# Layer 1's weights, biases and key tables prepared in the experts' block, in a pool of their own at the other end of SBUF

## The chip, the cores and the metric

The kernel runs on one core of one Trainium2 chip. The metric is the device time of one execution, in microseconds. Three runs of the kernel before took 2543.7, 2549.39 and 2550.09 us, the median is 2549.39 us. One more execution was taken with the hardware profiler. All rows of the trace below come from that one.

The engines are named as in the profile: PE (TensorE's matmuls), PEld (its weight loads), DVE (VectorE), ACT (ScalarE), POOL (GpSimd) and SP (SyncE, which here issues DMAs).

## The reference

The model has four layers over x of shape 4 x 512 x 128 (B, S, D). Each layer adds a cross attention onto a context of 77 tokens and then a feed-forward part. What matters here is the end of layer 0 and all of layer 1:

```python
x = x + _L0_ffn_ref(_layernorm(x), ln_gamma, ln_beta, Wr, W12, W3)       # 8 experts, top 2
x = x + _L1_xcond_ref(_layernorm(x), ctx_1024, ctx_1024, tau, delta, Wq, bq, Wk, ...)
x = x + _L1_ffn_ref(_layernorm(x), w1, conv_w, conv_b, w2)
x = x + _L2_xcond_ref(ctx_1024, _layernorm(x), _lenS2, condB_pt, W_a, W_c)
...
# _L1_ffn_ref: linear layers with ternary weights and quantised activations
scale = 1.0 / clip(mean(abs(w)), 1e-5);  wq = clip(round(w * scale), -1, 1) / scale
h = bit_linear(x, w1); h = depthwise_conv1d(h, conv_w, conv_b); h = silu(h); return bit_linear(h, w2)
# _L2_xcond_ref: mask = (idx < max(p_t-16, 0)) | (idx > min(p_t+16, src_len))
# gauss = exp(-(idx - p_t)**2 / 128); align = softmax(score) * gauss
```

Two things of this depend on the weights and on four numbers per batch alone, not on x. The first is layer 1's ternary weights, multiplied by the three taps of the convolution and turned, together with the convolution's bias. The second is layer 2's window: the mask, the bell `gauss`, and the keys W_a times context. The kernel calls the first `bit_weights` (L1165) and the second `window_tables` (L1386).

## The kernel before, in words

The work is cut into blocks, one after the other. In each, `with planned() as plan` collects pieces, and `Plan.run` writes them out in an order of its own when the block ends. A piece names the pieces it comes after, the PSUM banks or buffers it takes and uses, and a cost for each engine that may do it. Of all pieces that could start, the planner takes the one with the earliest start. Of those with one start it takes the one with the longest path of costs behind it, and it gives the piece to the engine that would be done first. Costs are in units of about 10 ns, and each engine has a fixed lag on top (30 for PE, 10 for DVE, 250 for a DMA). There are eight PSUM banks. A bank is held from the piece that takes it until the last piece that uses it has been written out. The result is a fixed order on each engine: every engine works through its own queue in that order and waits wherever an operand isn't ready.

The blocks, with their times in the trace:

- **Layer 0's cross attention and routing** (0 to about 164 us), inside `first_part`. POOL sends each token's row to the table `sent` by indirect DMA (`scatter`, L1017).
- **Layer 0's experts** (about 164 to 294 us), also in `first_part`, in the pool `m0w`. For each of eight experts SP fetches 640 rows (`xe`, L1048), PE turns them (L1104), ACT applies gamma and beta (`xTe`, L1559). Then come eight steps of two products (L1565, L1566), a Silu on ACT (L1569) and a product on DVE (`times`, L1572), five output products (L1583), a weighting on DVE (`ye`, L1131), and an indirect DMA by POOL that sends the rows to the table `back`. `xe`, `to` (the rows' destinations, L1089), `hT` and `ye` have two buffers each, so the third expert needs what the first has finished with. In the trace the experts go in pairs: sixteen steps, then ten output products. In this block stands also `context(plan, wp, 1)` (L614): the keys and values of layer 1's cross attention. It has no predecessors, so the planner puts it first.
- **Layer 1** (about 294 to 513 us), `middle_part`. `collect` (L1142) fetches the rows of `back` per batch (L1152) and adds them to x (L1158). For each batch follow the norm (`xa_st` L534, `xa_rs` L544 and L545, `xa_n` L550), the transposes (L568), their copy `xa_t` (L302), the queries (L683), the scores (L698, L703), their maxima on DVE (L711), the logits (L755, L757), the exponentials (L763), the sums and means (L773, L782), the quotient `shares` (L302) and the residual. Then come `bit_ffn`, `window_attention`, and the transposes into Y. The weights of `bit_ffn` and the tables of `window_attention` are made in the same block, in the pool `b1`, which is opened last.
- **The local transformer** (513 us to about 2250 us) and **layer 3** (the rest), which the diff doesn't touch.

What `bit_weights` does: SP loads w1, w2, the taps and the bias (L1178 to L1181). DVE splits the bias into three bf16 terms (`three_terms`, L321 to L328). `ternary` sums the absolute values (DVE L1203), spreads the sum over the partitions (PE L1206), and rounds (DVE L1209 to L1215). Three times DVE multiplies by a tap (`wj`, L1229), PE turns the result (L1233), and ACT or DVE copies it to w1T (L302). At last w2 is turned (L1245) and copied. What `window_tables` does: SP loads two small vectors (L1398, L1399). DVE computes bounds, mask and exponent (L1402 to L1415), ACT the bell (Exp, L1418), PE the keys (L1421), DVE their product with the mask (L1424).

Silu needs another activation table on ACT than Exp. The changes are ACT_TABLE_LOAD rows in the trace: one before the experts' first Silu, one before layer 1's first Exp.

A pool that is opened where an older one has been closed can be written only when everything in that older pool has been used for the last time.

Of the kernel before, what the change touches and what calls it, by code (L numbers as in the profile page):

```python
# [238 lines left out]
def tile_kernel(ctx: ExitStack, tc: tile.TileContext, A: dict, out: bass.AP):  # L239
# [922 lines left out]
        return last  # L1162


    def bit_weights(plan, mp):  # L1165

        w1, w2 = (mp.tile([128, NFC, 128], F32, name=f"bw{k}") for k in range(2))
        cw = mp.tile([128, NFC, 3], F32, name="cw")
        cb = mp.tile([128, FF], BF16, name="cb")
        w1T = mp.tile([128, 3, FF], F32, name="w1T")  # L1170
        w2b = mp.tile([128, NFC, 128], BF16, name="w2b")
        w2T = mp.tile([128, NFC, D], BF16, name="w2T")
        out_scale = mp.tile([128, 1], F32, name="out_scale")
        magic = mp.tile([128, 2], F32, name="magic")
        row = plan.buf(mp, [128, FF], F32, "cbrow", 1)

        def load(e):
            e.dma_start(w1, A["L1_ffn_w1"].rearrange("(c p) d -> p c d", p=128))  # L1178
            e.dma_start(w2, A["L1_ffn_w2"].rearrange("d (c f) -> d c f", f=128))
            e.dma_start(cw, A["L1_ffn_conv_w"].rearrange("(c p) o j -> p c (o j)", p=128))  # L1180
            e.dma_start(row.t, A["L1_ffn_conv_b"].partition_broadcast(128))  # L1181

        def magics(e):
            e.memset(magic[:, 0:1], MAGIC)
            e.memset(magic[:, 1:2], -MAGIC)

        loaded = plan.add(load, takes=[row], Q=200)
        done = [plan.add(magics, G=30, V=20)]
        for k in range(4):
            def terms(e, k=k):  # L1190
                at = slice(128 * k, 128 * k + 128)
                three_terms(cb[:, at], row.t[:, at], mp, [128, 128], e)

            done.append(plan.add(terms, [loaded], uses=[row], V=120))

        def ternary(w, scale):

            part = mp.tile([128, 1], F32, name=f"tn_part{w is w2}")
            r = mp.tile([128, 1], F32, name=f"tn_r{w is w2}")
            bank = plan.bank()  # L1200

            def total(e):
                e.tensor_reduce(part, w, AX.XY, ALU.add, apply_absolute_value=True)  # L1203

            def spread(e):
                e.matmul(bank.view(128, 1), ones, part, start=True, stop=True)  # L1206

            def rounded(e):
                e.tensor_scalar(scale, bank.view(128, 1), 1.0 / (FF * D), 1e-5, ALU.mult, ALU.max)  # L1209
                e.reciprocal(r, scale)  # L1210
                e.tensor_scalar(w, w, r, MAGIC, ALU.mult, ALU.add)
                e.tensor_scalar(w, w, MAGIC, 1.0, ALU.subtract, ALU.min)
                e.tensor_scalar(w2b if w is w2 else w, w, -1.0, None, ALU.max)
                if w is w2:
                    e.tensor_scalar(scale, scale, 1.0 / 254.0, None, ALU.mult)  # L1215

            p = plan.add(total, [loaded], V=68)
            p = plan.add(spread, [p], takes=[bank], PE=15)
            return plan.add(rounded, [p], uses=[bank], V=200)

        m1 = mp.tile([128, 1], F32, name="tn_m")
        t1, t2 = ternary(w1, m1), ternary(w2, out_scale)

        for j in range(3):
            bank, wj = plan.bank(), plan.buf(mp, [128, NFC, D], F32, "wj")

            def tap(e, j=j, wj=wj):
                for c in range(NFC):
                    e.tensor_scalar(wj.t[:, c], w1[:, c], m1, cw[:, c, j : j + 1], ALU.mult, ALU.mult)  # L1229

            def flip(e, bank=bank, wj=wj):
                for c in range(NFC):
                    e.transpose(bank.view(128, NFC, 128)[:, c], wj.t[:, c], ident)  # L1233

            def out(e, j=j, bank=bank):
                copy(e, w1T[:, j], bank.view(128, FF))

            p = plan.add(tap, [t1], takes=[wj], V=112)
            p = plan.add(flip, [p], takes=[bank], uses=[wj], PE=54)
            done.append(plan.add(out, [p], uses=[bank], S=59, V=69))  # L1240
        bank = plan.bank()

        def flip2(e):
            for c in range(NFC):
                e.transpose(bank.view(128, NFC, 128, dtype=BF16)[:, c], w2b[:, c], identb)  # L1245

        def out2(e):
            copy(e, w2T, bank.view(128, NFC, 128, dtype=BF16))

        p = plan.add(flip2, [t2], takes=[bank], PE=26)  # L1250
        done.append(plan.add(out2, [p], uses=[bank], S=59, V=69))
        return done, w1T, w2T, cb, out_scale, magic
# [130 lines left out]
        return last  # L1383


    def window_tables(plan, kp):  # L1386

        pt = kp.tile([128, B], F32, name="pt")
        leni = kp.tile([128, B], I32, name="leni")
        end, st, pe = (kp.tile([128, B], F32, name=n) for n in ("end", "st", "pe"))  # L1390
        keep, gauss, wk = (kp.tile([128, B, SK], F32, name=n) for n in ("keep", "gauss", "wk"))
        neg = kp.tile([128, B, SK], BF16, name="neg")
        above = kp.tile([128, SK], F32, name="above")
        idx = cst[:, C_IDX : C_IDX + SK]
        bank = plan.bank()

        def load(e):
            e.dma_start(pt, A["condB_pt"].partition_broadcast(128))  # L1398
            e.dma_start(leni, A["_lenS2"].partition_broadcast(128))  # L1399

        def bounds(e):
            e.tensor_copy(end, leni)  # L1402
            e.tensor_scalar(st, pt, 16.0, 0.0, ALU.subtract, ALU.max)
            e.tensor_scalar(pe, pt, 16.0, None, ALU.add)
            e.tensor_tensor(end, pe, end, ALU.min)

        def inside(e, b):
            e.tensor_scalar(keep[:, b], idx, st[:, b : b + 1], None, ALU.is_ge)
            e.tensor_scalar(above, idx, end[:, b : b + 1], None, ALU.is_le)
            e.tensor_tensor(keep[:, b], keep[:, b], above, ALU.mult)  # L1410
            e.tensor_scalar(gauss[:, b], idx, pt[:, b : b + 1], None, ALU.subtract)

        def outside(e):
            e.tensor_scalar(neg, keep, 1.0, cst[:, C_BIG : C_BIG + 1], ALU.subtract, ALU.mult)
            e.tensor_tensor(gauss, gauss, gauss, ALU.mult)  # L1415

        def bell(e):
            e.activation(gauss, gauss, AF.Exp, scale=-1.0 / 128.0)  # L1418

        def keys(e):  # L1420
            e.matmul(bank.view(128, B, SK), wT[:, 12], ctxT, start=True, stop=True)  # L1421

        def kept(e):
            e.tensor_tensor(wk, bank.view(128, B, SK), keep, ALU.mult)  # L1424

        p = plan.add(bounds, [plan.add(load, Q=80)], V=64)
        for b in range(B):
            p = plan.add(lambda e, b=b: inside(e, b), [p], V=96)
        p = plan.add(outside, [p], V=90)
        done = [plan.add(bell, [p], S=46)]  # L1430
        q = plan.add(keys, takes=[bank], PE=60)
        done.append(plan.add(kept, [p, q], uses=[bank], V=48))
        return done, wk, neg, gauss
# [79 lines left out]
        return last  # L1513


    def first_part():

        with ExitStack() as es:
            pool = lambda name, bufs=2: es.enter_context(tc.tile_pool(name=name, bufs=bufs))
# [4 lines left out]
            with tc.tile_pool(name="xw0", bufs=2) as wp, planned() as plan:  # L1524
# [10 lines left out]
                for e0 in range(E):  # L1535
# [7 lines left out]
                    for g in range(3):  # L1543
# [10 lines left out]

                        p = plan.add(flip, [loaded], takes=[bank], uses=[raw if g < 2 else raw3], PE=58)
                        plan.add(out, [p], uses=[bank], S=60, V=69)
            with tc.tile_pool(name="m0w", bufs=2) as wp, planned() as plan:
                def turn_in(e, dst, t):
                    e.activation(dst, t, AF.Identity, scale=col(R_GAM), bias=col(R_BET))  # L1559
# [25 lines left out]
                sends, issued = experts(  # L1585
                    plan, wp, sent[:1], back[0], CAP0, [], turn_in, hidden, down, R.issued
                )
                context(plan, wp, 1)
            return issued

    def middle_part(issued, Y):

        with ExitStack() as es:
            yp = es.enter_context(tc.tile_pool(name="y0", bufs=2))
            wp = es.enter_context(tc.tile_pool(name="xw1", bufs=2))
            mp = es.enter_context(tc.tile_pool(name="b1", bufs=1))
            with planned() as plan:
                start = collect(plan, yp, back[0], issued, [])
                last = cross_attention(plan, wp, 1, [], start)
                last = bit_ffn(plan, wp, bit_weights(plan, mp), [[p] for p in last])  # L1600
                last = window_attention(plan, wp, window_tables(plan, mp), last)
                for b in range(B):


# [502 lines left out]
    with tc.tile_pool(name="y", bufs=1) as yp:  # L2107
        Y = []
        for b in range(B):
            y = yp.tile([128, S + 1], F32, name=f"y{b}", tag=f"y{b}")  # L2110
            G.memset(y[64:128, 0:1], 0.0)
            Y.append(y)
        with ExitStack() as es:
            open_cross(es)
            middle_part(first_part(), Y)
        local_transformer(Y)
    with ExitStack() as es:
        open_cross(es)
# [20 lines left out]
```

## Time and profile before

| what | value |
| --- | --- |
| median of the runs | 2549.39 us (2543.7 to 2550.09) |
| the profiled execution | 2504.74 us |
| its span, first to last instruction | 2503.0 us |
| mean granted clock of PE | 0.958 |
| PE, DVE, POOL, ACT busy | 90%, 72%, 62%, 50% |
| first xe fetched | 166.81 us |
| first output row sent to `back`, last one sent | 193.35 us, 292.33 us |
| first rows of `back` fetched by SP | 294.53 us |
| local transformer's first load on SP | 513.18 us |

A row of a timeline has the start, the length, the engine, the line of the code, the operation, what is written and read, the shape, and a count. In brackets stands how long the engine had been idle before, and what ended that. A row of stages has the busy time of each engine in that stretch, with the number of instructions in parentheses, then the granted clock of PE as a share of full speed, the DMA engines' share, and GB/s. The profiled execution is about 45 us shorter than the median of the runs.

### The profile page before, as it was taken

The page shows a single profiled execution, that of the slowest core. Times are in us where ns is not written, and L with a number is a line of the kernel's source. Part 1 is how long each engine was busy: PE and PEld are TensorE (multiplying, and loading weights), DVE is VectorE, ACT ScalarE, POOL GpSimd, SP SyncE. Part 2 cuts the span into 40 slices and gives each one's busy share as a digit, 9 for nine tenths or more (in the row PEclk, how much of TensorE's full clock was granted, in tenths as well). Part 3 has the DMA queues.
Part 4 walks back from the last instruction along what each step waited for, and adds up shares of the span by engine and source line. Part 5 has one row for each costly group of instructions (what it writes and reads, how often), then busy time and mean ns, then how long its engine had stood idle before and what let it go on. Part 6 is the DMA issues. An engine that isn't in the chain of part 4 may idle for free.

```text
span 2503.0 us, 87683 instructions
## 1 busy us (share of the span) xinstructions
PE 2254.2 (90%) x37341; PEld 1471.1 (59%) x37341; DVE 1791.1 (72%) x4016; ACT 1243.5 (50%) x2185; POOL 1542.9 (62%) x2613
## 2 busy tenths in 40 slices
PE   7969789968999999999999999999999999978776
PEld 3547534535666666666666666666666666634455
DVE  5543475757887888888888888888888888737522
ACT  3623134534565655556555555565555655514322
POOL 2333312357777777777778777777777777712543
PEclk9979889989999999999999999999999999979888
DMA  6211200026211121111211121111211111111023
GB/s 160 87 31 38 70 1 2 1 58 138 73 35 28 35 69 35 33 28 35 71 34 35 28 78 31 30 32 28 78 32 29 35 28 35 33 29 50 27 68 90
DMA packets 134305, 116.21 MB, mean 46 GB/s; under 512 B 29505, under 2 KB 102700, under 8 KB 133916
## 3 DMA queue, kind: packets, MB, share of 16 engines
q1 hardware_dynamic: 128373, 102.81, 15.8%
q0 software_dynamic: 4608, 7.35, 0.9%
q8 instruction: 296, 4.85, 0.8%
q14 instruction: 93, 0.76, 0.1%
q10 hardware_dynamic: 935, 0.43, 0.1%
HBM read 42.84 MB, written 21.52 MB: 26 GB/s over the span
## 4 chain that ended last, share of the span: by engine, by line
PE 57%; DVE 20%; issue 8%; POOL 7%; ACT 5%; DMA 3%; SPq 1%; ACTq 0%; POOLq 0%; DVEq 0%
PE ps_tr L582 9%; PE ps_mm L1774 8%; PE ps_av L1938 4%; PE ps_tr L1853 4%; PE ps_av L1914 4%; PE ps_sc L1883 3%; DVE rc L1784 3%; DVE rs L1787 3%; DVE ss L1796 3%; PE ps_sc L1984 3%; PE ps_sc L1996 3%; PE ps L1312 2%; DVE P L1894 2%; PE ps L773 2%; DVE la_mx L1893 2%
## 5 line engine op out<-in xcount | busy, mean ns | idle before, releaser
L1797 POOL TENSOR_TENSOR rc<-rc,rs 128x512 f32<-128x512 f32 x384 | 488.6, 1276 | 230.6 <-DVE rs L1787 186.5
L1774 PE MATMUL ps_mm<-wqk,y 128*128 128x512 f32 x768 | 397.5, 600 | 11.0 <-DVE rs L1787 7.8
L1818 POOL TENSOR_TENSOR rc<-rc,rn_y 128x512 f32<-128x512 f32 x384 | 388.8, 1044 | 7.5
L1784 DVE TENSOR_TENSOR rc<-ps_mm,tabs 128x512 f32<-128x512 f32 x384 | 262.4, 683 | 160.9 <-ACT sq L1776 145.6
L1899 ACT ACTIVATE P<-P 128x1024 f32<-128x1024 f32 x96 | 101.4, 1057 | 422.3 <-DVE P L1894 422.3
L1776 ACT ACTIVATE sq<-ps_mm 128x512 f32<-128x512 f32 x384 | 231.0, 602 | 152.3 <-PE ps_mm L1774 104.4
L1787 DVE TENSOR_TENSOR rs<-ps_mm,tabs 128x512 f32<-128x512 f32 x384 | 261.5, 681 | 5.9 <-POOL rc L1797 5.8
L1796 DVE TENSOR_REDUCE ss<-sq 128x8 f32<-128x512 f32 x384 | 259.4, 676 | 0.0
L582 PE MATMUL ps_tr<-cst,rc 128*128 128x128 f32 x1536 | 211.0, 281 | 6.8 <-POOL rc L1818 4.6
L1914 PEld LDWEIGHTS ps_av<-v,PT 64*32 64x32 f32 x12288 | 137.8, 105 | 127.3 <-PE ps_tr L582 54.9
L1938 PE MATMUL ps_av<-aT,wo 128*128 128x128 f32 x1536 | 198.6, 282 | 4.7 <-issue 4.7
L1938 PEld LDWEIGHTS ps_av<-aT,wo 128*128 128x128 f32 x1536 | 179.2, 191 | 14.7 <-issue 6.0
L582 PEld LDWEIGHTS ps_tr<-cst,rc 128*128 128x128 f32 x1536 | 165.4, 141 | 26.2 <-POOL rc L1818 5.7
L1883 PE MATMUL ps_sc<-kT,qT 64*32 64x64 f32 x12288 | 146.7, 225 | 34.5 <-issue 26.9
L1914 PE MATMUL ps_av<-v,PT 64*32 64x65 f32 x12288 | 168.8, 225 | 7.0 <-DVE attn L1924 5.4
L1883 PEld LDWEIGHTS ps_sc<-kT,qT 64*32 64x32 f32 x12288 | 140.2, 105 | 45.2 <-issue 30.9
L1017 POOL DMA_INDIRECT back<-ye,to x80 | 77.6, 970 | 141.7 <-DVE ye L1131 102.5
L1774 PEld LDWEIGHTS ps_mm<-wqk,y 128*128 128x128 f32 x768 | 124.9, 193 | 61.0 <-issue 44.7
L763 ACT ACTIVATE P<-ps,deltaT 77x512 f32<-77x512 f32 x192 | 115.1, 682 | 59.1 <-PE ps L757 58.9
L1830 ACT COPY kT<-ps_tr 128x512 f32<-128x512 f32 x192 | 103.3, 589 | 82.3 <-PE ps_tr L582 82.1
L1830 ACT COPY qT<-ps_tr 128x512 f32<-128x512 f32 x192 | 103.2, 589 | 76.8 <-PE ps_tr L582 74.4
L1924 DVE TENSOR_TENSOR attn<-ps_av,la_den 128x512 f32<-128x512 f32 x192 | 132.8, 691 | 6.6
(392 smaller groups left out, 4453.7 us busy)
## 6 DMA issues: line engine op xcount, KB each, us to landing
v<-v SPq DMA_DIRECT2D x432, 65.0 KB
v<-v SPq DMA_DIRECT2D x96, 195.0 KB
wqk<-in_L_ffn_Wqkv_dram SPq DMA_DIRECT2D x24, 256.0 KB
sent<-xn SPq DMA_DIRECT2D x2, 2210.0 KB
xe<-sent SPq DMA_DIRECT2D x16, 260.0 KB
back<-xn SPq DMA_DIRECT2D x2, 2048.0 KB
raw<-in_L_ffn_W_dram SPq DMA_DIRECT2D x8, 512.0 KB
yb<-back SPq DMA_DIRECT2D x16, 256.0 KB
```

The lines of the kernel that those rows point to most:

```text
L582: PE.transpose(t[:, i], src[:, i], ident)
L1774: PE.matmul(t, lhs, T.w[2 * kind + c], start=True, stop=True)
L1776: SC.activation(sq, t, AF.Square)
L1784: V.tensor_tensor(a, t, bc(T.tabs[:, 2 * kind, tt], [128, 8, LD], 1), ALU.mult)
L1787: V.tensor_tensor(r.rearrange("p h (x d) -> p h x d", x=2), t.rearrange("p h (x d) -> p h x d", x=2)[:, :, ::-1], bc(T.tabs[:, 2 * kind + ...
L1796: V.tensor_reduce(T.ss[:, kind, 8 * c : 8 * c + 8], sq, AX.X, ALU.add)
L1797: G.tensor_tensor(a, a, r, ALU.add)
L1818: G.tensor_tensor(a, a, bc(y[:, o : o + 8], [128, 8, LD], 2), ALU.mult)
L1830: SC.copy(t[:, 4 * c : 4 * c + 4, lead:], to_features(T.rot[kind, c].rearrange("p (k x) d -> p k (x d)", x=2)),)
L1883: PE.matmul(T.banks[32 * w : 32 * w + 32, z, k], T.qT[r, k, 32 * w : 32 * w + 32], T.kT[r, k, 32 * w : 32 * w + 64], start=False, stop=Tru ...
L1914: PE.matmul(T.means[32 * w : 32 * w + 32, x0, k], T.PT[r, 4 * g + k, 32 * w : 32 * w + 32], (T.v1 if w % 2 else T.v2)[r, x0, 4 * g + k], s ...
L1938: PE.matmul(t, T.wo[:, c], T.aT[:, c], start=(c == 0), stop=(c == 7))
```

## The change

The diff does four things.

1. `bit_weights` and `window_tables` are called in the experts' block, after `experts`, and no longer in layer 1's. Layer 1 gets their tiles and an empty list of predecessors.
2. What layer 1 reads later stays in the pool `b1`, which is now opened between the two blocks of `first_part`, on the right side of SBUF (pools are otherwise stacked from the left), and is closed after layer 1. This holds for cb, w1T, w2T, out_scale, magic, wk, neg, gauss and the small vectors.
3. What is needed only while preparing moves into the experts' pool `m0w`. This holds for the raw weights, the taps, w2b, the bias row, wj, the parts of `three_terms`, keep and above.
4. `context(plan, wp, 1)` gets predecessors: those of the fifth send from the end, which is the first send of the last expert.

```diff
-    def bit_weights(plan, mp):
+    def bit_weights(plan, mp, wp):
-        w1, w2 = (mp.tile([128, NFC, 128], F32, name=f"bw{k}") for k in range(2))
-        cw = mp.tile([128, NFC, 3], F32, name="cw")
+        w1, w2 = (wp.tile([128, NFC, 128], F32, name=f"bw{k}", bufs=1) for k in range(2))
+        cw = wp.tile([128, NFC, 3], F32, name="cw", bufs=1)
...
-        w2b = mp.tile([128, NFC, 128], BF16, name="w2b")
+        w2b = wp.tile([128, NFC, 128], BF16, name="w2b", bufs=1)
...
-        row = plan.buf(mp, [128, FF], F32, "cbrow", 1)
+        row = plan.buf(wp, [128, FF], F32, "cbrow", 1)
...
-                three_terms(cb[:, at], row.t[:, at], mp, [128, 128], e)
+                three_terms(cb[:, at], row.t[:, at], wp, [128, 128], e)
...
-            bank, wj = plan.bank(), plan.buf(mp, [128, NFC, D], F32, "wj")
+            bank, wj = plan.bank(), plan.buf(wp, [128, NFC, D], F32, "wj")
...
-    def window_tables(plan, kp):
+    def window_tables(plan, kp, wp):
...
+        keep = wp.tile([128, B, SK], F32, name="keep", bufs=1)
...
+        above = wp.tile([128, SK], F32, name="above", bufs=1)
...
-    def first_part():
+    def first_part(kept):
...
+            kp = kept()
             with tc.tile_pool(name="m0w", bufs=2) as wp, planned() as plan:
...
-                context(plan, wp, 1)
-            return issued
+                weights = bit_weights(plan, kp, wp)
+                tables_ = window_tables(plan, kp, wp)
+
+                context(plan, wp, 1, sends[-5].after)
+            return issued, weights, tables_
...
-            mp = es.enter_context(tc.tile_pool(name="b1", bufs=1))
...
-                last = bit_ffn(plan, wp, bit_weights(plan, mp), [[p] for p in last])
-                last = window_attention(plan, wp, window_tables(plan, mp), last)
+                last = bit_ffn(plan, wp, ([],) + weights[1:], [[p] for p in last])
+                last = window_attention(plan, wp, ([],) + tables_[1:], last)
...
-            middle_part(first_part(), Y)
+            kept = lambda: es.enter_context(tc.tile_pool(name="b1", bufs=1, side="right"))
+            middle_part(*first_part(kept), Y)
```

More of the change, by code (lines that the diff above doesn't have):

```diff
@@ L1390, in window_tables @@
         end, st, pe = (kp.tile([128, B], F32, name=n) for n in ("end", "st", "pe"))
-        keep, gauss, wk = (kp.tile([128, B, SK], F32, name=n) for n in ("keep", "gauss", "wk"))
+        keep = wp.tile([128, B, SK], F32, name="keep", bufs=1)
+        gauss, wk = (kp.tile([128, B, SK], F32, name=n) for n in ("gauss", "wk"))
         neg = kp.tile([128, B, SK], BF16, name="neg")
-        above = kp.tile([128, SK], F32, name="above")
+        above = wp.tile([128, SK], F32, name="above", bufs=1)
         idx = cst[:, C_IDX : C_IDX + SK]
@@ L1587, in first_part, with middle_part @@
                 )
-                context(plan, wp, 1)
-            return issued
-    def middle_part(issued, Y):
+                weights = bit_weights(plan, kp, wp)
+                tables_ = window_tables(plan, kp, wp)
+                context(plan, wp, 1, sends[-5].after)
+            return issued, weights, tables_
+    def middle_part(issued, weights, tables_, Y):
         with ExitStack() as es:
```

## The prediction

> **What bounds the kernel now.** I read the page first (PE busy 90% of the span), then cut the span into stages, because the change touches only 164 to 513 us. The stages by engine, in us: stretch, length, then busy time and instruction count of PE, PEld, DVE, ACT, POOL, then the granted clock.
>
> ```profile
> 170.00:199.00 29.00, 28.34 (x145) 22.26 (x146) 11.05 (x25) 10.53 (x21) 5.67 (x7) 0.92 0.07 20
> 288.40:294.50 6.10, 0.79 (x2) 0.30 (x2) 0.18 (x1) 0.00 (x0) 3.90 (x4) 0.70 0.07 21
> 294.50:304.40 9.90, 1.13 (x4) 1.00 (x4) 4.44 (x16) 0.00 (x0) 1.27 (x2) 0.50 0.79 215
> 304.40:325.00 20.60, 17.23 (x74) 6.83 (x78) 16.43 (x56) 3.69 (x6) 2.88 (x4) 0.50 0.14 38
> 325.00:352.00 27.00, 22.58 (x228) 9.80 (x220) 25.14 (x96) 11.39 (x19) 4.79 (x6) 0.94 0.01 2
> 352.00:472.00 120.00, 118.31 (x1157) 56.35 (x1153) 74.75 (x232) 57.89 (x97) 32.79 (x63) 0.98 0.01 2
> ```
>
> A pair of experts (170 to 199) is PE's, with DVE and ACT idle over 60%. Between the stages (288 to 304) PE is empty while the last scatters and the fetch of their rows run. From 304 to 352 DVE has 41.6 of 47.6 us and PE runs at half clock until 325: here DVE sets the pace. From 352 PE is full, so an earlier arrival there should reach the end of layer 1 undiminished.
>
> Next the timeline where layer 1 starts (start, length, engine, line, what; in brackets the wait and its releaser):
>
> ```profile
> 303.75 0.69 DVE L1158 TENSOR_TENSOR x<-x,yb 128x512 f32<-128x512 f32 x1 [2.34 <-DMA yb<-back]
> 304.36 1.11 DVE L550 TENSOR_SCALAR xa_n<-x,xa_mv,xa_rs 128x128 f32<-128x128 f32 x4
> 306.16 0.59 ACT L302 COPY xa_t<-ps 128x512 f32<-128x512 f32 x1 [26.96 <-DMA yb<-back]
> 358.50 0.59 ACT L302 COPY shares<-ps 128x512 f32<-128x512 f32 x1 [3.02 <-PE ps L804]
> ```
>
> Batch 0's norm is ready for DVE at 301.7 (POOL's xa_rs ends) but stands behind batch 1's rows in DVE's queue. From batch 0's first xa_t to its shares pass 52.3 us. The same two lines in layer 0's cross attention:
>
> ```profile
> 24.86 0.59 ACT L302 COPY xa_t<-ps 128x512 f32<-128x512 f32 x1 [1.77 <-PE ps L568]
> 60.62 0.59 ACT L302 COPY shares<-ps 128x512 f32<-128x512 f32 x1 [3.42 <-PE ps L804]
> ```
>
> Here it takes 35.8 us, at a granted clock of 1.00. The step from batch 0's shares to batch 1's is the same in both (25.7 us, and 384.39 - 358.50 = 25.9), so shares is a fair mark of progress. The 16.5 us between 52.3 and 35.8 are preparation on DVE plus the cold clock.
>
> **What leaves layer 1's start.** DVE, from its groups between 290 and 400 us: taps 3.4; three_terms 0.9+1.2+1.1+0.9+1.2+1.4+1.4 = 8.1; the two ternaries 5.0; copies to w1T 1.3; tables 6.0; together 23.8 us. PE: sums 1.2, flips of the taps 1.7, of w2 0.4 = 3.3 us. Two PSUM banks go too: the window keys' (288.6 to 351.5, when L1424 has read it) and the second ternary's (301.5 to about 331.4). SP loses six DMA issues (295.61 to 298.5) that stand between batch 0's rows and batch 1's, so batch 1's are asked for about 3 us earlier.
>
> Start: with both batches' rows there, DVE does x0, x1, both statistics and then xa_n of batch 0 at about 303.0 instead of 304.36, so xa_t is at 304.7, 1.4 us sooner. Then 35.8 us as in layer 0, plus the cold clock. PE idle from about 292 to 302 falls to 0.50 again. Here I weigh the Trainium skill ("TensorE: Matmul & The Clock Gate", Part 1: The HAM clock gate): about 3.4 us of sustained activity bring the full clock. By the rule PE, dense from about 309 once DVE doesn't break it, is warm at 313. By the row it was 84% busy from 304 to 325 and stayed at 0.50 all that time. Cold matmuls cost about 1.85 times the hot ones (the query pair 2.08 against 1.13 us). By the rule about 8 cold busy us lose 4 us; if the row repeats, 17 lose 8. I take 5, nearer the rule, because the breaks the row shows are waits for DVE. Shares of batch 0 then come at 304.7 + 35.8 + 5 = 345.5, not 358.5: **-13**. I carry -12.5; ends -4 (head start 1.4 plus PE's 2.4 us of preparation before 352) and -20.
>
> **What the experts get.** The same 23.8 and 3.3 us, six loads, and a Silu-Exp-Silu turn on ACT. The steady state there:
>
> ```profile
> 187.11 0.49 DVE L1572 TENSOR_TENSOR hT<-ps,hT 128x320 f32<-128x320 f32 x1 [0.58 <-PE ps L1566]
> 187.58 0.44 ACT L1569 ACTIVATE hT<-ps 128x320 f32<-128x320 f32 x1 [0.64 <-PE ps L1565]
> ```
>
> - Loads: on SP behind the first two xe fetches, so from about 168.6, landed by 174; the third fetch isn't due until 196.24. Nobody queued behind them: 0. If w1 came late, DVE's first product (174.43) would wait a microsecond or two.
> - DVE: each 1.07 us step of PE uses 0.49 of DVE. The planner takes `times` first, its path being longer, so preparation goes into the gaps; a piece is 0.7 to 1.9 us. With two banks a step and seven free (the window keys hold one) PE can run some 2 to 3 us ahead, so a single piece shouldn't stop it: 0 to +2, I take 0.3. Without that cover it is 23.8.
> - PE: the planner ranks all experts' products above spreads and flips, so these go where PE would wait: the turn between pairs, below. At one turn PE waits 0.82 us for xTe (201.61) and 0.98 for xe (205.01); over the first turns that hides about 2 of the 3.3 us: +1.3 (0 to 3.3).
> - The turn between pairs is a chain through DVE:
>
> ```profile
> 226.54 5.31 SPq L1048 DMA_DIRECT2D xe<-sent  x2
> ...
> 230.78 0.17 DVE L1089 CAST to<-xe 128x5 uint32<-128x5 f32 x1 [1.59 <-DMA back<-ye,to]
> 230.86 0.60 DVE L1131 TENSOR_SCALAR ye<-ps,xe 128x128 f32<-128x128 f32 x2
> ...
> 234.72 0.63 PE L1104 MATMUL ps<-cst,xe 128*128 128x128 f32 x4 [0.35 <-DMA xe<-sent]
> ```
>
> The last two ye free the xe buffer whose refill PE waits for. A preparation piece ahead of them delays the refill by up to 1.9 us: +1.2 (0 to 4, at two turns).
> - ACT: bell's Exp leaves Silu's table and must come back to it:
>
> ```profile
> 172.14 1.28 ACT L1569 ACT_TABLE_LOAD   x1
> 173.43 0.44 ACT L1569 ACTIVATE hT<-ps 128x320 f32<-128x320 f32 x1
> ```
>
> By this row two loads and bell (0.46) take 3.0 us. The skill's "ScalarE: Activation LUTs", section Table sets: the hidden batching unit, speaks against the change: keep functions of one set together, since a switch costs about 2.7 us; that makes 5.8. In the row Silu starts 10 ns after the load with no further gap, so 3.0; PE's lead hides about 2: +0.7 (0 to 3.5 by the rule).
>
> Sum **+3.5** (0 to +13).
>
> **Context.** At its old place it ended at 163.5, under the last scatter, and the first xe was fetched at 166.81: nothing is saved. At the new place it follows the last products (288.6): values about 2.6 and keys 0.8 us on a warm PE, kT 1.15, masks about 1.6 on DVE, over by 295, before the first x add (297.28). Queued behind its waits on PE and DVE is only layer 1, which waits for the scatters (to 294.5). Cost 0, about 6 if that cover were gone. POOL loses one mask (1.06 us) nobody waits for. The pool on the other side takes away the wait for the experts' pool (DVE's magic waited 6.0 us for the scatters), which held nothing else.
>
> **Sum.** -12.5 + 3.5 = **-9 us**, against the profiled execution: 2504.74 (span 2503.0), to 2495.7. The runs shown have a median of 2549.39, 1.8% more; the local transformer's 1,730 us are untouched, so I carry the same microseconds over: **2540**.
>
> **Rivals.**
> 1. DVE was only busy, not the limit (0.26). For: PE was 84% busy in both halves of 304 to 352, and a cold clock stretches it whatever DVE does. Against: the wait for xa_n, and layer 0's 35.8 us. Gain about 5, experts +4: 2548.
> 2. Layer 1 starts as briskly as layer 3's cross attention (0.17): there xa_t at 2259.58 and shares at 2283.50 are 23.9 us apart, with all rows present and eight banks free. Against: here rows arrive by DMA and the clock is cold. Gain 20, experts +3: 2532.
> 3. Slower (0.07): DVE's fixed order becomes the experts' limit in the first two pairs (172 to 229), `times` and ye standing behind pieces of up to 1.9 us while seven banks run out. With a share f of the 23.8 us exposed, the change is -12.5 + 3.3 + 23.8f: above zero from f = 0.39; at f = 0.8 it is +10: 2559. Against: DVE idles 18 of 29 us there.
> 4. The change doesn't do what it says: ranked lowest, flips and copies slip past the last expert. They would run at 288 to 302, where PE is empty, still before the first use at 387: same time, inside the main case.
>
> **How the numbers follow.** Main case 0.50 (-4 to -14, of that 0.36 beyond -7.6). About 0.3%, 7.6 us, is what a measurement of this kernel can tell from no change. Faster: 0.36 + 0.17 = 0.53. Slower 0.06, from rival 3. The rest, 0.41, is same. Range 2531 to 2552: rival 2 to -18 and rival 1 to +3, leaving out about 0.06 below and 0.08 above.
>
> **What would show it.** Right: no line of bit_weights or window_tables after the experts; batch 0's shares 38 to 44 us after its xa_t; clock back at 1.00 before 320; the last ye 2 to 6 us later; ACT with two more table loads. Wrong: shares still 50 us after xa_t (rival 1); DVE gap-free and PE waiting for hT in the first pairs (rival 3). What would overturn most is the planner ordering layer 1 anew, so that the window attention's tail (472 to 513, PE 32.6 of 41 us busy) comes out differently; nothing in the profile says which way.

## The result and the profile after

| | before | changed |
| --- | --- | --- |
| median of 11 runs each | 2551.61 us (2543.7 to 2563.99) | 2539.33 us (2528.36 to 2552.27) |
| the profiled execution, its span | 2504.74, 2503.0 us | 2544.82, 2543.0 us |
| granted clock of PE in it | 0.958 | 0.944 |

The ratio is 0.9941, 95% interval 0.992 to 0.9962: 0.59% faster, some 15 us (0.0059 x 2551.6). The two profiled executions can't be subtracted, because the chips differ: the kernel before takes 2556 us on one, 2510 on a second and 2559 on a third. The first profile of before (2504.74 us) looks like the second chip's, that of the changed kernel like the first's. So below I compare stages within one chip where I can, and say where I don't. The ratio of vector_back below leaves out one execution of 3647.77 us, at a granted clock of 0.554. The stages of the changed kernel's first profile, with the columns as in the prediction:

```profile
327.00:333.07 6.07, 1.47 (x7) 0.72 (x6) 3.66 (x13) 0.52 (x2) 3.05 (x3) 0.76 0.01 1
333.07:342.90 9.83, 1.09 (x4) 0.68 (x4) 5.59 (x20) 0.00 (x0) 2.02 (x2) 0.50 0.71 206
342.90:350.60 7.70, 6.56 (x33) 2.73 (x34) 6.59 (x27) 1.69 (x3) 4.65 (x6) 0.50 0.04 13
350.60:379.40 28.80, 26.94 (x363) 13.38 (x366) 18.10 (x50) 16.28 (x27) 3.06 (x5) 1.00 0.00 1
379.40:499.40 120.00, 117.17 (x1105) 58.38 (x1100) 77.38 (x242) 60.62 (x110) 41.30 (x74) 0.98 0.01 2
```

From the first xa_t (342.9) to batch 0's shares (379.5) DVE is now busy for 24.7 of 36.5 us (68%); in the kernel before it was 43.6 of 52.3 us (83%). PE has the full clock from 350.6 to 379.4, and 0.98 on average in the 120 us after. The timeline of the same start:

```profile
341.12 1.12 DVE L550 TENSOR_SCALAR xa_n<-x,xa_mv,xa_rs 128x128 f32<-128x128 f32 x4 [0.94 <-POOL xa_rs L545]
342.92 0.59 ACT L302 COPY xa_t<-ps 128x512 f32<-128x512 f32 x1 [13.41 <-DMA yb<-back]
379.46 0.58 ACT L302 COPY shares<-ps 128x512 f32<-128x512 f32 x1
```

Batch 0's norm waits for POOL alone, and xa_t to shares takes 36.5 us. In the experts, the first turn between pairs:

```profile
216.41 1.28 ACT L1419 ACT_TABLE_LOAD   x1
219.55 0.35 DVE L1131 TENSOR_SCALAR ye<-ps,xe 128x128 f32<-128x128 f32 x1
...
221.71 0.60 DVE L1131 TENSOR_SCALAR ye<-ps,xe 128x128 f32<-128x128 f32 x2
...
227.85 1.09 PE L1104 MATMUL ps<-cst,xe 128*128 128x128 f32 x4 [2.46 <-DMA xe<-sent]
...
234.34 1.28 ACT L1572 ACT_TABLE_LOAD   x1
```

Four `three_terms` pieces stand among the ten ye, one of them between the first two rows of ye shown here; the refilled xe comes 2.46 us late for PE, and ACT changes its table twice.

### The profile page after: what moved, and what is told of

Read it like the earlier page. It is cut to its first block, busy times and chain, and to the rows that moved or that the text cites. A ratio compares the mean times of both kernels' runs of the same rounds, so it can differ in the third digit from the quotient of the medians.

```text
span 2543.0 us, 87670 instructions
## 1 busy us (share of the span) xinstructions
PE 2287.4 (90%) x37341; PEld 1489.2 (59%) x37341; DVE 1789.3 (70%) x4010; ACT 1245.4 (49%) x2186; POOL 1549.6 (61%) x2620
## 4 chain that ended last, share of the span: by engine, by line
PE 54%; DVE 24%; issue 7%; ACT 6%; POOL 4%; DMA 2%; another core or an unknown queue 1%; SPq 1%; ACTq 0%; POOLq 0%; DVEq 0%
PE ps_tr L582 8%; PE ps_mm L1779 8%; DVE rc L1789 4%; DVE rs L1792 4%; DVE ss L1801 4%; PE ps_av L1919 3%; PE ps_av L1943 3%; PE ps_tr L1858 3%; PE ps_sc L1989 3%; PE ps_sc L2001 3%; PE ps_sc L1888 2%; DVE P L1899 2%; PE ps L773 2%; DVE la_mx L1898 2%; PE ps L782 2%
## 5 line engine op out<-in xcount | busy, mean ns | idle before, releaser
L1888 PEld LDWEIGHTS ps_sc<-kT,qT 64*32 64x32 f32 x12288 | 139.8, 105 | 40.9 <-issue 27.0
```

What stands on the lines that cost most here:

```text
L1888: PE.matmul(T.banks[32 * w : 32 * w + 32, z, k], T.qT[r, k, 32 * w : 32 * w + 32], T.kT[r, k, 32 * w : 32 * w + 64], start=False, stop=Tru ...
```

## The experiments

Three chips were used, called first, second and third. A stage is measured by marks that every kernel has. The experts' block runs from the first xe fetch to the first yb fetch. Layer 1 runs from there to the local transformer's first load, and is cut at batch 0's xa_t and at its shares. All in us, from one profile each; the ratio is to the kernel before on the same chip.

| kernel | chip | ratio | experts | layer 1 | to xa_t | xa_t to shares | shares to end |
| --- | --- | --- | --- | --- | --- | --- | --- |
| tie_alone | first | 0.9999 [0.9982, 1.0016] | 139.4 | 217.4 | 12.1 | 50.8 | 154.6 |
| changed, first profile | | 0.9941 [0.992, 0.9962] | 143.4 | 198.7 | 9.9 | 36.5 | 152.3 |
| again | first | 0.9946 [0.9926, 0.9965] | 143.5 | 198.7 | 9.8 | 36.5 | 152.3 |
| untied | first | 0.9947 [0.9929, 0.9964] | 141.3 | 200.2 | 9.8 | 38.8 | 151.5 |
| no_prep | first | 0.9921 [0.9898, 0.9944] | 140.2 | 200.4 | 9.7 | 39.0 | 151.7 |
| changed_here | third | 0.9932 [0.9906, 0.9957] | 142.1 | 197.9 | 9.9 | 36.5 | 151.5 |
| prep_later | third | 0.9987 [0.9969, 1.0006] | 139.8 | 214.1 | 11.5 | 40.8 | 161.8 |
| matmuls_back | third | 0.9937 [0.9913, 0.9961] | 141.9 | 198.4 | 9.6 | 36.5 | 152.2 |
| before_again | second | | 128.9 | 220.6 | 12.5 | 53.5 | 154.7 |
| loads_early | second | 0.9991 [0.998, 1.0003] | 128.6 | 217.8 | 11.3 | 56.1 | 150.4 |
| tables_stay | second | 0.9949 [0.993, 0.9969] | 130.8 | 204.1 | 10.1 | 43.8 | 150.2 |
| vector_back | second | 0.9974 [0.9961, 0.9986] | 130.4 | 204.0 | 13.8 | 35.1 | 155.1 |
| both_back | second | 1.0 [0.9985, 1.0014] | 132.3 | 217.4 | 13.9 | 54.6 | 148.9 |

A ratio below 1 is faster than the kernel before; in brackets is its 95% interval. The expectations name theories by letters (A, B and so on) anew for each run.

My theory at first was the prediction's: VectorE set layer 1's pace, and 24 us of its work have gone. The rivals were the other things that went (banks, transposes, loads), and the context's tie.

**again**: no edit.

> The changed kernel once more, for a second profile. In its first profile layer 1 was 20 us shorter than before and the experts' block (first xe fetch to first yb fetch) 15.7 us longer (143.4 for 127.7 us); some 9 us of that lay in the turns after the second, third and fourth expert pair, where the last ye scalings came 2.86 us apart. Theory A, those steps belong to the changed program: the experts' block is 140 to 146 us again, with the steps. Theory B, they belong to that one execution (its clock was throttled early): the block is 130 to 137 us, without them. Time by either 2535 to 2545 us, as measured.

The same block and the same late steps came again (143.5 us), as theory A had it. But theory A's "they belong to the changed program" fell with the next runs, which have them too.

**untied**

```diff
-                context(plan, wp, 1, sends[-5].after)
+                context(plan, wp, 1)
```

> The changed kernel with the context's pieces free again (no predecessor), so they run at the start of the experts. Theory A (the context at the tail costs nothing; it ends before the first x add): 2536 to 2544 us, the same as the changed kernel. Rival (the tie brings the 2.86 us steps or lengthens the tail): 2526 to 2532 us, and the experts' block 6 to 9 us shorter than the changed kernel's.

0.9947 beside 0.9946: the tie costs nothing that can be measured.

**tie_alone** (kernel before)

```diff
-                context(plan, wp, 1)
+                context(plan, wp, 1, sends[-5].after)
```

> The kernel before with the context's tie alone; pool and preparation stay in layer 1. Theory A (the gain is the preparation leaving layer 1, the tie costs nothing): 2549 to 2555 us, as before, experts' block 127 to 129 us. Rival 1 (the tie costs 9 us in the experts): 2558 to 2562 us. Rival 2 (the tie is itself a gain, for it takes the context's work from the first pair): 2545 to 2548 us, the first pair's hidden steps 1 to 3 us shorter.

0.9999, so theory A holds for the time. Its block of 127 to 129 us was wrong: it was 139.4, with the same late ye steps (start, length, engine, line):

```profile
250.85 0.35 DVE L1131 TENSOR_SCALAR ye<-ps,xe 128x128 f32<-128x128 f32 x1 [0.94 <-PE ps L1583]
253.70 0.35 DVE L1131 TENSOR_SCALAR ye<-ps,xe 128x128 f32<-128x128 f32 x1 [2.49 <-PE ps L1583]
256.57 0.35 DVE L1131 TENSOR_SCALAR ye<-ps,xe 128x128 f32<-128x128 f32 x1 [2.53 <-remote]
```

Two ye come 2.86 us after the one before, where 0.89 is usual; preparation stands nowhere near. As the time is that of before, this kernel serves as the kernel before on the first chip.

**no_prep**

```diff
+    def zero_weights(plan, kp):          # nine memsets on GpSimd, in place of all the preparation
...
-                weights = bit_weights(plan, kp, wp)
-                tables_ = window_tables(plan, kp, wp)
+                weights, tables_ = zero_weights(plan, kp)
```

> The changed kernel without the preparation: layer 1's weights, biases and key tables are left out and their tiles set to constants by GpSimd at the start of the experts (so layer 1 computes on zeros); no loads, no table switch for the bell, no pieces on VectorE and TensorE. Theory A (layer 1 gains 20 us and the experts pay 5 to 15 us for it): 2525 to 2532 us, experts' block 127 to 130 us, layer 1 (first yb fetch to the next layer's weight load) 198 to 200 us as in the changed kernel. Rival (the experts hide the preparation, and their longer block comes from elsewhere): 2536 to 2542 us, block near 140 us.

Layer 1 is the changed kernel's within 1.7 us, the experts' block tie_alone's within 0.8. So the preparation costs the experts about 3 us, and leaving it out altogether makes layer 1 no shorter than moving it does. The ratios (0.9921 and 0.9946) don't separate the two kernels.

**before_again**: the kernel before, no edit.

> The kernel before once more, for a second profile: its first profiled execution took 2504.7 us, some 47 us less than its median. Theory A (that execution had an unusually high clock, and the kernel with the context's tie alone shows the ordinary state): first xe fetch at 180 to 190 us for 166.8, experts' block 138 to 141 us for 127.7, with two ye steps of 2.86 us at the end of each expert pair, layer 1 217 to 219 us. Rival (the tie is what lengthened the block): block 127 to 131 us again, ye steps as in the first profile.

It ran on the second chip and looked like the first profile of before: block 128.9, layer 1 220.6. So theory A's guess about one odd execution and the rival's about the tie are both wrong: the chip makes the difference. Here the end of an expert pair has no such steps:

```profile
230.30 0.35 DVE L1131 TENSOR_SCALAR ye<-ps,xe 128x128 f32<-128x128 f32 x1 [0.54 <-PE ps L1583]
232.31 0.60 DVE L1131 TENSOR_SCALAR ye<-ps,xe 128x128 f32<-128x128 f32 x2
```

**vector_back**

```diff
+                zw, zt = vector_only(plan, zp)      # VectorE's pieces of both functions, on scratch tiles
-                last = bit_ffn(plan, wp, ([],) + weights[1:], [[p] for p in last])
+                last = bit_ffn(plan, wp, (zw,) + weights[1:], [[p] for p in last])
...                                                  # zt goes to window_attention in the same way
```

> The changed kernel with VectorE's part of the preparation put back into layer 1, as work on scratch tiles (same shapes, same planner costs, what follows waits for it as before; 23 us in all); no loads, no TensorE transposes, no PSUM banks. Theory A (layer 1 gains because VectorE, its limit, is freed): layer 1 goes back to 212 to 217 us from 199, the time to 2553 to 2558 us. Rival 1 (the freed banks, the transposes, the loads between the rows, the earlier start of the clock): layer 1 stays at 199 to 204 us, the time at 2541 to 2546 us.

Neither range held: layer 1 204.0, and 4 us of what it lost lie before xa_t, where batch 0's norm now went to GpSimd behind the fill of my scratch tiles. From xa_t to shares it took 35.1 us, beside 36.5 for the changed kernel (on the other chips). The planner did not put all of the work there: of 22 us that can be told apart in the trace, 4.8 lie before xa_t, 11.5 between xa_t and shares, and 5.9 later; in the first profile of before it was 22.1 between the two. Still, VectorE is busier here than in before (32.7 of 35.1 us, 93%), and the stretch is 17 us shorter. The main theory falls: a busy VectorE alone doesn't make the stretch long, and its work put back cost some 3 us after shares (155.1 for 152).

**loads_early** (from the changed kernel; all but the loads goes back to layer 1)

```diff
-                weights = bit_weights(plan, kp, wp)
-                tables_ = window_tables(plan, kp, wp)
+                got = early_loads(plan, kp)         # the six dma_starts, nothing else
...
+                last = bit_ffn(plan, wp, bit_weights(plan, kp, zp, got), [[p] for p in last])
```

> The six loads alone moved into the experts, with their tiles in the pool on the other side; all the rest of the preparation stays in layer 1. Theory A (VectorE's work is the gain): layer 1 215 to 218 us, time 2552 to 2556 us, as the kernel before. Rival (the loads, between batch 0's rows and batch 1's on the queue and landing ahead of the first piece, are a good part): layer 1 205 to 211 us, time 2543 to 2549 us.

217.8, ratio 0.9991: the loads aren't it, nor is the pool's place, which this kernel has as the changed one does.

**tables_stay** (`window_tables` goes back to layer 1)

```diff
-                tables_ = window_tables(plan, kp, wp)
...
+                last = window_attention(plan, wp, window_tables(plan, zp, zp), last)
```

> Weights and biases prepared in the experts, the key tables in layer 1 (6.2 us of VectorE's 23.8 us, one matmul and the bell's exponential; so no table switch in the experts). Theory A (gain in proportion to VectorE's work): layer 1 203 to 205 us, experts' block 1 to 2 us shorter than the changed kernel's 143.4, time 2543 to 2546 us. Rival (the table switches cost more than the tables' work in layer 1): 2536 to 2539 us, block 139 to 140 us.

204.1 us is in theory A's range, but the explanation below (both_back) leads there too, so this run does not decide. The two table loads less brought the block no visible gain (130.8, where the others of this chip with preparation in it have 130.4 and 132.3).

**changed_here**: no edit.

> The changed kernel, for a profile beside the next two kernels on one chip. On the second chip, where the kernel before took 2510 us, no profile of it is to be had yet; its experts' block there should be 130 to 132 us (with VectorE's work put back it was 130.4) and its layer 1 198 to 202 us, ratio 0.993 to 0.996; on the first chip 143.4 and 198.7 us as before.

It came to a third chip, much like the first; so no changed kernel was profiled on the second.

**prep_later** (kernel before)

```diff
...                                                  # VectorE's and TensorE's first pieces take `then`
+                then = last[0].after[:1]            # batch 0's projection
-                last = bit_ffn(plan, wp, bit_weights(plan, mp), [[p] for p in last])
-                last = window_attention(plan, wp, window_tables(plan, mp), last)
+                last = bit_ffn(plan, wp, bit_weights(plan, mp, then), [[p] for p in last])
+                last = window_attention(plan, wp, window_tables(plan, mp, then), last)
```

> The kernel before with its preparation left in layer 1, and its pool too; only its pieces on VectorE and TensorE now have batch 0's projection as predecessor, so that none of it stands ahead of batch 0's shares in any queue (its loads start as before). Theory A (layer 1 lost its time to the 24 us of VectorE's work as such, wherever it stands): layer 1 213 to 218 us, ratio 0.997 to 1.000. Theory C (it lost it to where the work stood: ahead of batch 0's chain on VectorE, and TensorE's queue held by pieces that wait for it, while later VectorE has idle time): layer 1 200 to 206 us, the experts' block as before, ratio 0.992 to 0.995, as fast as the changed kernel or faster.

Batch 0's shares came early (40.8), then layer 1 lost it all again: from batch 1's shares to batch 2's 41.4 us passed, where it is 28.8 in the changed kernel. By its numbers theory A held (0.9987, layer 1 214.1), and theory C fell: a later place doesn't help.

**matmuls_back**

```diff
+                zw, zt = matmuls_only(plan, zp)     # 16 transposes, 2 sums, key matmul, 7 banks, copies
-                last = bit_ffn(plan, wp, ([],) + weights[1:], [[p] for p in last])
+                last = bit_ffn(plan, wp, (zw,) + weights[1:], [[p] for p in last])
...
```

> The changed kernel with the other part of the preparation put back into layer 1, on scratch tiles: sixteen transposes, two sums over partitions, one key matmul, their seven PSUM banks and copies, none of it waiting for VectorE's work. Theory B (banks, transposes and copies are the gain): layer 1 208 to 214 us, ratio 0.997 to 1.000. Theory C (only their waiting for VectorE's pieces ahead of batch 0 costs): layer 1 200 to 204 us, ratio 0.994 to 0.996.

198.4: as in the changed kernel. PE's part alone costs nothing.

**both_back**: the two edits together.

> The changed kernel with both parts of the preparation put back into layer 1 at once, each on its own scratch tiles, and no piece of the one waiting for a piece of the other (in the kernel before a VectorE piece waits for a TensorE piece, which waits for a VectorE piece, and the next copy waits again). Alone, VectorE's part made layer 1 204.0 us long and TensorE's 198.4, beside 198 to 199 for the changed kernel and 217 to 221 for the kernel before. Theory D (the sum of the work counts, VectorE's time and the seven banks together): layer 1 212 to 220 us, batch 0's shares 60 us or more after the first yb fetch, ratio 0.998 to 1.001. Theory E (the links count: the queues of two engines held by waits for each other): layer 1 202 to 206 us, the shares at 48 to 52 us, ratio 0.995 to 0.998.

Theory D held in its numbers: 217.4 us, ratio 1.0. Each part alone leaves xa_t to shares at 35 to 37 us, both make it 54.6. That much is shown. Why two parts that cost nothing there alone cost 18 us together is the question, and one PSUM bank stands out. PE does the window keys (`wT[:, 12]`) before layer 1's rows are there, and VectorE's `kept` reads the bank. The matmul and its reader, in both_back, matmuls_back, tie_alone and prep_later:

```profile
297.36 1.36 PE L1290 MATMUL ps<-ctxT,wT 128*128 128x308 f32 x2 [1.43 <-DVE kT L639]
347.38 0.47 DVE L1293 COPY mzgauss<-ps 128x308 f32<-128x308 f32 x1
```

```profile
318.19 1.36 PE L1216 MATMUL ps<-ctxT,wT 128*128 128x308 f32 x2 [1.81 <-DVE kT L639]
322.24 0.48 DVE L1219 COPY zgauss<-ps 128x308 f32<-128x308 f32 x1 [2.92 <-POOL zgauss L1175]
```

```profile
325.34 1.36 PE L1421 MATMUL ps<-ctxT,wT 128*128 128x308 f32 x2 [1.58 <-DVE kT L639]
382.45 0.47 DVE L1424 TENSOR_TENSOR wk<-ps,keep 128x308 f32<-128x308 f32 x1
```

```profile
380.75 0.79 PE L1421 MATMUL ps<-ctxT,wT 128*128 128x308 f32 x2
426.54 0.47 DVE L1424 TENSOR_TENSOR wk<-ps,keep 128x308 f32<-128x308 f32 x1
```

The bank is held for 50 us in both_back and 57 in tie_alone, through all of batch 0, because the reader stands last in VectorE's low-ranked chain. In matmuls_back there is no such chain, and it is free after 4 us. In prep_later it is held for 46 us later on, and there the later batches lose the time (their shares at 403.4 and 444.8). In vector_back nobody takes it in layer 1. The nearest to a test of the bank is tables_stay, on vector_back's chip: there the bank is held for 36 us (read 34.5 us into layer 1), with about 4.3 us of VectorE's preparation between xa_t and shares, and the stretch is 43.8. Vector_back has 11.5 us of such work there and no bank held, and 35.1. In both_back all other pieces on PE have been copied out 6.7 us after the first yb fetch, so from there on the bank is the one piece of work in which it differs from vector_back. (The order on the engines differs too, because the planner counts banks.) The kernel before holds a second bank early as well, the second ternary's (in tie_alone from 335.3 to 362.7); no run tests that one.

How one bank can do that is read from the code and the order, not shown by a run of its own: a set of scores takes four banks and a set of logits four more, so with seven one set waits until the other has been read. Two lists from the traces show what scores (L698) waited for, 20 to 66 us into layer 1 ("issue" is time in which the engine waited for nothing that the profile shows), first both_back, then vector_back (us, times):

```profile
  issue: 7.6, 11
  ACT P L763: 2.5, 6
  DVE maxes L711: 1.1, 1
```

```profile
  issue: 5.4, 9
  ACT P L763: 1.0, 2
```

No score reads P. What it waits for is that ACT has read the logits out of its bank. One set of scores in both_back shows it, bank by bank, beside one in vector_back:

```profile
340.93 0.29 PE L698 MATMUL ps<-delta,first 32*128 32x308 bf16 x1 [0.76 <-ACT P L763]
341.51 0.29 PE L698 MATMUL ps<-delta,first 32*128 32x308 bf16 x1 [0.28 <-ACT P L763]
342.08 0.29 PE L698 MATMUL ps<-delta,first 32*128 32x308 bf16 x1 [0.28 <-ACT P L763]
342.66 0.29 PE L698 MATMUL ps<-delta,first 32*128 32x308 bf16 x1 [0.28 <-ACT P L763]
```

```profile
345.70 0.31 PE L698 MATMUL ps<-delta,first 32*128 32x308 bf16 x4
```

In sum the two lists of waits differ by 4.8 us, so they alone do not make up the 19.5 us. Batch 0's four sets of logits start at 33.9, 40.2, 47.5 and 51.7 us in both_back, and at 28.8, 30.8, 36.5 and 39.3 in vector_back. The same stretch by engine, vector_back and then both_back, 20 to 60 us into layer 1 (columns as above):

```profile
322.98:342.98 20.00, 17.51 (x212) 8.42 (x214) 19.53 (x65) 10.85 (x17) 3.88 (x6) 1.00 0.00 1
342.98:362.98 20.00, 17.24 (x266) 8.42 (x262) 17.92 (x66) 9.67 (x17) 2.05 (x3) 1.00 0.01 2
```

```profile
318.74:338.74 20.00, 16.61 (x136) 7.23 (x128) 18.92 (x65) 6.48 (x10) 4.40 (x6) 0.83 0.00 1
338.74:358.74 20.00, 16.98 (x148) 6.66 (x144) 12.26 (x49) 8.39 (x14) 0.00 (x0) 0.64 0.00 1
```

VectorE is fuller in vector_back, the faster one. In both_back PE issues 284 instructions for 478, and its clock falls. The clock is the rival that stays. Here is the whole stretch from xa_t to shares in vector_back, both_back, tie_alone and the changed kernel:

```profile
316.78:351.91 35.13, 30.23 (x378) 15.23 (x382) 32.69 (x109) 16.41 (x27) 6.38 (x9) 0.93 0.01 1
312.60:367.23 54.63, 47.43 (x406) 20.18 (x406) 38.67 (x135) 19.39 (x32) 6.42 (x9) 0.71 0.01 1
340.01:390.77 50.76, 42.79 (x396) 18.89 (x400) 43.41 (x153) 18.49 (x30) 7.65 (x10) 0.83 0.04 11
342.92:379.46 36.54, 33.56 (x396) 16.11 (x400) 24.67 (x75) 18.03 (x30) 7.71 (x10) 0.89 0.01 3
```

By the part of the clock not granted (an estimate: length times one less the clock) both_back loses 15.8 us and vector_back 2.5, that is 13 of the 19.5 us between them; tie_alone loses 8.6 and the changed kernel 4.0, that is 5 of their 14. So for the change itself the clock is the smaller part. How much is the clock's own and how much comes of PE waiting stays open. Nor was the remedy tried that would settle the bank: layer 1's preparation left where it was, with the key matmul put right ahead of its reader.

## Why the prediction was right or wrong

The sum was -9 us. On the first and third chip the changed kernel's layer 1 is 19.0 us shorter than tie_alone's (217.4 less the mean 198.4 of three profiles), and its experts' block 3.4 longer than the mean of tie_alone and prep_later (143.0 less 139.6). That makes -15.6; the ratios give 14 to 17 (0.9946, 0.9941, 0.9932). The direction and the small terms were right; the large term was too small (-12.5 for -19.0), and its cause was wrong. That the total came within 7 us is in good part luck.

- **Head start, -1.4**: 12.1 to 9.9 us, -2.2. Right in kind.
- **xa_t to shares, to layer 0's 35.8 plus 5 for the cold clock**: 36.5, not 41, from 50.8 in tie_alone: -14.3 where the step had -11.5 (52.3 to 40.8). 6.56 us of PE's work in it fell at 0.50, which loses about 3.3 us by estimate, and still it took no more than 36.5: layer 0's pace was no floor.
- **"From 352 PE is full, so an earlier arrival there should reach the end of layer 1 undiminished"**: it even grew, by 2.5 us (154.6 to a mean of 152.0).
- **"Here DVE sets the pace"**: the step that failed. VectorE was 87% busy from 304 to 352, but in vector_back it is 93% busy from xa_t to shares, and the stretch takes 35.1 us. Nor does PE's part cost anything alone (36.5). Only both together do (54.6). The prediction named the window keys' bank with its times (288.6 to 351.5) and gave it no price. That bank, held because its reader stands late in VectorE's queue, is the likeliest link between the two parts, but its share of the 14 us is not shown, and some 5 of them are the lower clock by the estimate above. The figure came out near by luck: it was taken from layer 0's pace and not from the cause that it named.
- **PE's 3.3 us in layer 1**: nothing (matmuls_back 198.4 for 197.9).
- **The clock**: the rule of the Trainium skill ("TensorE: Matmul & The Clock Gate", Part 1) has 3.4 us of sustained activity; the row had 20. In the changed kernel it took 9 us from PE's first transpose (341.67) to 350.6; the loss of 3.3 us is near the 4 that the prediction worked out from the rule, and less than the 5 taken. But the reason given, that breaks kept the clock low, is not borne out: in before_again PE was busy for 11.6 of the 12 us from 316 to 328, and its clock stayed at 0.50. There the full clock came 32 us after the first yb fetch, here 17.5.
- **Experts, +3.5**: +3.4. Of its parts, the loads stood behind one xe fetch, not two: the second was issued behind them, at 193.15. PE didn't wait for it. ACT's two more table loads came, at 1.28 us each. The turn's delay through ye came too (2.46 us at xe). The 2.86 us steps are in every turn of tie_alone anyway, and may cover part of it. The sums and flips did not wait for the turn, as the prediction had it: two sums ran at 197.06 and a tap's flips at 208.32, among the first pair's products.
- **Context, 0**: right; 0.9999 with the tie alone, within 0.17%.
- **Rivals**: the first ("DVE was only busy, not the limit") had the cause right as to VectorE, but took from it that little could be gained. The second (-20 and +3) had the two sizes almost to the microsecond (-19.0 and +3.4), for another reason. In the third, PE would wait for hT; the first pair's sixteen steps took 21.7 us for 19.6 in tie_alone (first product to last), far from its break-even, which is 9 us of VectorE's work exposed.

## What to carry to other kernels

Put removed work back part by part, and then together: in layer 1 one part cost 6 us (4 of them by the fill of its scratch tiles), the other nothing, both 19 (with the same 4). Count PSUM banks over time as you count an engine's work: a bank that an early matmul has filled, with a reader ranked last on a busy engine, is the suspect here, and the prediction had it on its list at no price. An engine that is 87% busy isn't yet the limit; see whether the waits around it end on it or on a buffer. And compare stages by fixed marks within one chip before you subtract two profiles.

## What the hardware showed unexpectedly

- Chips differ by 1.8 to 1.9% on the same program: the kernel before has medians of 2556.2 and 2558.7 us on two, 2510.5 on another, with granted clocks in the profiles of 0.943 to 0.952 on the two and 0.955 to 0.961 on the other. Ratios agreed between the first and third chip (0.9946, 0.9932).
- On the two slower chips each expert pair (but for the first one where preparation stands among its ye) ends with two steps of about 2.86 us between ye, where PE's records run on without a gap; on the other, in the kernel before, the first three pairs have one larger gap of 1.8 to 2.4 us. From the first ye to the last group of ye the four pairs take 43.5 us in tie_alone and 33.1 in before_again, which is the 10 us by which the experts' block is longer there (139.4 for 128.9). The cause is open.
- PE's clock came back after 9 us of work in one start and after 20 in another of the same stage, and stayed at 0.50 in a third through 12 us in which PE was 97% busy (before_again, columns as in the prediction):

```profile
316.00:328.00 12.00, 11.60 (x57) 4.19 (x56) 8.92 (x29) 2.54 (x4) 1.26 (x2) 0.50 0.00 1
```
